# Side steps spaced apart beside a scan, wider rotation over PSUM banks, and delta's ranks computed in four column groups

## The chip, the cores and the metric

The kernel runs on one core of a Trainium2 chip. TensorE (PE) multiplies matrices into PSUM, VectorE (DVE), ScalarE (ACT) and GpSimd (POOL) work on tiles in SBUF (the first two also in PSUM), and SyncE (SP) issues all the DMAs of this kernel on one queue. Each engine runs its instructions in the order in which they stand in its own list and waits, by semaphores, for what other engines make. The metric is the time of one execution on the device in microseconds; lower is better. Runs of the same program are compared by their medians.

## The reference, cut to what matters

Sixteen images of 256 channels and 32 x 32 positions (1024 tokens) pass two layers, each behind a group norm and each with a residual. The first is attention with four heads of 32 and a feed-forward; the second is a gated selective scan with 512 inner channels and 64 states for each.

```python
# layer 0, x += f(gn(x))
tok = gn(x) + pos
q, k, v = split(layernorm(tok) @ w_qkv)
tok = softmax(q k^T * scale) v @ w_out + b_out + tok
tok = gelu(layernorm(tok) @ w_ff1 + b_ff1) @ w_ff2 + b_ff2 + tok
# layer 1, x += f(gn(x)) with pos = rel_h + rel_w added
ctx = sigmoid(conv3(xs) + gate_b)
u, z = split(xs @ in_proj_w.T)
u = silu(causal_depthwise_conv4(u))
dt, Bm, Cm = split(u @ x_proj_w.T, [16, 16 + 64])
delta = softplus(dt @ dt_proj_w.T + dt_proj_b)
h = exp(delta * A) * h + (delta * u) * Bm      # per token, 512 channels x 64 states
y = (h * Cm).sum(states) + u * D
out = (y * silu(z)) @ out_proj_w.T * ctx
```

The recurrence in `h` goes over the 1024 tokens one after another and is the bulk of the arithmetic: 512 x 64 rows of 1024 steps for each image.

## The kernel before, in words

**The scan.** A tile of 128 partitions holds two channels with 64 states each. Tokens are halved into two blocks of 512 (`t`), channels into four groups of 128 (`k`), each into four parts (`q`) of eight units (`i`). So an image has 256 units, and a unit is two scan instructions of 128 x 512 on DVE (`scan`, L893). What a unit needs is made by other engines ahead of it:

- `load` (L842) brings delta times u to all 64 states by DMA, six units ahead, into one of seven buffers `dub`.
- `inputs` (L868) multiplies it by B on POOL (L871), four units ahead.
- `decay` (L873), two units ahead: two PE matmuls (L880) spread three bfloat16 pieces of delta over the states into PSUM tiles `a`, and ACT takes the exponential in place (L883). There are four such tiles, so the matmuls of unit n + 2 write where unit n was read from.
- `outputs` (L917) follows each eight units as a Python generator that is advanced once in every unit: many small PE matmuls (L927) sum h times C over the states into the tile `yb`, ACT copies the half (L935), PE transposes it (L939), ACT copies it again (L947), and four small DMAs (L954) store it in `ys`. The matrix `cd`, made of C, is filled by ACT in `spread_c` (L902).

**The side work.** While image b is scanned, image b + 1 is prepared (`first_norm`, L321; `attention_layer`, L337; `scan_inputs`, L567), and image b - 1 is finished (`gate_and_store`, L773: add u times D, multiply with z, output projection, context gate, residual, store). These are generators too. Each yields a number, its share, after every small step. The main loop (L973) adds a rate to `due` in every unit, and while `due` is positive takes the next step and subtracts its share. The rate is the sum of all shares over the 247 units that may take steps: 247.8 for a preparation, 26.6 more for a gate stage. Whatever is left runs six units before the image ends.

In a unit the loop writes: the load, POOL's product, two scans, the decays of n + 2, side steps, one step of each running `outputs`. At the end of the program (L1022 on) PE, ACT, DVE and POOL are bound to exactly this order by dependencies without semaphores. SP's queue is not bound, and its DMAs stand in the order that the tile framework's scheduler gives them, near this one.

**PSUM.** Eight banks: four for `a` (pool `aps`), one for `yb`, one for the attention's sums `av` (pool `accp`), two for all other products of the side work (pool `mm`). `psum` (L98) hands out the two in turn while a scan runs beside.

**Steps that the change touches.** `group_norm` (L230), `layer_norm` (L271): sums over channels by a matmul with a constant matrix, then Ln and Exp on ACT for the inverse root, then a multiplication on DVE (L267, L306). Scores, softmax and values of attention (L406, L474, L482, L462), projections q and k (L374). z with its tanh (L597 to L617), u with its four taps (L642), the context gate (L651), then dt, B and C (L692 on): for each half of the tokens four accumulating matmuls with 16 columns for dt and four with 128 for B and C. For delta, `begin` multiplies the 16 rows of dt with `w_dt` for each 128 channels (L716), and `begin`, `more` and `rest` make the softplus in small pieces on ACT and DVE (L714 to L765), which ends with three bfloat16 pieces stored to `dps` (L763).

## Time and profile before

| what | us |
|---|---|
| runs shown, median (lowest to highest of 3) | 13563.83 (13536.5 to 13569.5) |
| profiled execution, its own time | 13520.45 |
| its span, first to last instruction | 13518.5 |
| span up to the first scan (image 0 prepared alone) | 376.9 |
| image 0, from its first scan to image 1's | 801.3 |
| image 4, the same | 834.8 |
| from the last image's first scan to its last | 645.4 |
| after the last scan's start | 47.3 |
| busy: DVE, PE, POOL, ACT | 12165.9, 10686.8, 9761.5, 7916.0 |
| scans on DVE (8192 instructions) | 9618.0 |
| mean granted clock of PE, as a share of full | 0.768 |

An engine's busy time is the sum of its instructions; what is left of the span is idle time. In the lists of groups a row has the line, the engine, the operation, the tiles written and read with their sizes, the count, the busy time, the mean of one instruction, and the idle time of the engine just before these instructions with what ended it. In the busy time by windows each row is a stretch of the span, its length, the busy time of PE, PE's weight loads, DVE, ACT and POOL, the granted clock of PE, the share of time in which the DMA engines worked, and GB/s. Matmuls overlap and their ends are modelled, so a PE near its whole window is close to full and no more exact than that.

### The profile page before, as it was taken

How to read it: one execution, taken by the hardware profiler on the slowest of the kernel's cores; microseconds unless marked ns; L12 is line 12 of the kernel's file. 1: busy time of each engine (PE TensorE's matmuls, PEld its weight loads, DVE VectorE, ACT ScalarE, POOL GpSimd, SP SyncE). 2: the span in 40 equal slices, each digit the busy share in tenths (PEclk: the TensorE clock that was granted, in tenths of full speed). 3: DMA queues.
4: the chain of work that ended last, by engine and by line, in shares of the span. 5: the costliest groups of instructions: out<-in, count | busy, mean ns of one | idle time of the engine just before them, and what ended most of it. 6: DMA issues, size and time to landing. Idle time of an engine off the chain costs nothing. (4 is left out here: it accounts for less than half of the span.)

```text
span 13518.5 us, 429250 instructions
## 1 busy us (share of the span) xinstructions
PE 10686.8 (79%) x186800; PEld 5389.6 (40%) x186800; DVE 12165.9 (90%) x11652; ACT 7916.0 (59%) x13941; POOL 9761.5 (72%) x4118
## 2 busy tenths in 40 slices
PE   7787878878787787877878778787787878878767
PEld 3343344433444334443344433434444344433434
DVE  3899999899998999999999898999999999989998
ACT  3666665656655565555656556566465665656654
POOL 0777767777777777767777677776777767777697
PEclk8786877868788686876868778687786877868777
DMA  1566566565665666656666566655666566665666
GB/s 64 202 205 234 197 212 218 203 227 203 208 217 200 228 205 213 212 201 223 208 223 205 198 222 206 235 199 199 220 207 234 193 205 220 206 231 198 209 233 224
DMA packets 1001896, 2820.85 MB, mean 209 GB/s; under 512 B 175810, under 2 KB 319427, under 8 KB 1000004
## 3 DMA queue, kind: packets, MB, share of 16 engines
q1 hardware_dynamic: 1000004, 2793.39, 60.5%
q8 instruction: 1460, 23.92, 0.7%
q14 instruction: 432, 3.54, 0.1%
HBM read 2514.18 MB, written 261.62 MB: 205 GB/s over the span
## 5 line engine op out<-in xcount | busy, mean ns | idle before, releaser
L871 POOL TENSOR_TENSOR dub<-dub,bt 128x1024 f32<-128x1024 f32 x4096 | 9706.4, 2386 | 3702.5 <-DMA dub<-dus 3218.5
L883 ACT ACTIVATE a<-a,acol 128x512 f32<-128x512 f32 x8192 | 5063.6, 659 | 3830.4 <-PE a L880 3800.3
L893 DVE TENSOR_TENSOR_SCAN h<-a,last,dub 128x512 f32<-128x512 f32 x4096 | 4927.0, 1260 | 129.1 <-issue 88.0
L893 DVE TENSOR_TENSOR_SCAN h<-a,dub 128x512 f32<-128x512 f32 x4096 | 4691.0, 1199 | 281.1 <-issue 160.7
L880 PE MATMUL a<-pieces,pick 48*128 48x512 bf16 x8192 | 2983.3, 468 | 2447.9 <-DVE h L893 2371.4
L927 PEld LDWEIGHTS yb<-h,cd 128*32 128x32 f32 x131072 | 2568.5, 136 | 1945.6 <-issue 1700.1
L927 PE MATMUL yb<-h,cd 128*32 128x64 f32 x131072 | 2967.1, 259 | 28.8 <-issue 19.7
L880 PEld LDWEIGHTS <-pick 48*128 48x128 bf16 x8192 | 521.6, 96 | 2607.9 <-issue 2396.6
L406 PE MATMUL s_ps<-k,q 32*64 32x512 f32 x4096 | 890.4, 719 | 59.2 <-DVE mx L387 58.3
L939 PEld LDWEIGHTS yb<-turn,y 128*16 128x16 f32 x32768 | 408.7, 119 | 993.6 <-ACT y L935 493.2
L935 ACT COPY y<-yb 128x256 f32<-128x256 f32 x1024 | 383.3, 374 | 718.3 <-PE yb L927 714.3
L387 DVE TENSOR_REDUCE mx<-s_ps 128x1 f32<-128x512 f32 x1024 | 643.4, 669 | 24.4 <-PE s_ps L406 22.2
L939 PE MATMUL yb<-turn,y 128*16 128x32 f32 x32768 | 538.2, 212 | 103.2 <-ACT y L935 99.4
L474 PE MATMUL st_ps<-sp 33*128 33x512 f32 x2048 | 598.0, 627 | 14.1 <-ACT pt L482 13.9
L462 PE MATMUL av<-pt,vv 128*64 128x512 f32 x2048 | 577.3, 642 | 5.5 <-ACT sums L451 3.3
L482 ACT ACTIVATE pt<-st_ps 128x512 f32<-128x512 f32 x1024 | 556.7, 604 | 40.0 <-PE st_ps L474 38.8
L660 PE MATMUL g_ps<-w,xp 128*128 128x256 f32 x1536 | 447.4, 447 | 0.0
L406 PEld LDWEIGHTS s_ps<-k,q 32*64 32x64 f32 x4096 | 206.8, 148 | 580.1 <-DVE mx L387 540.3
L660 PEld LDWEIGHTS g_ps<-w,xp 128*128 128x128 f32 x1536 | 389.5, 328 | 100.5 <-issue 77.4
L645 DVE SCALAR_TENSOR_TENSOR u<-up,cwh,u 128x1024 f32<-128x1024 f32 x192 | 341.0, 1776 | 32.8 <-ACT u L637 32.5
L819 PE MATMUL m_ps<-w,xs 128*128 128x256 f32 x1024 | 310.4, 451 | 12.3 <-DVE xs L794 12.3
L819 PEld LDWEIGHTS m_ps<-w,xs 128*128 128x128 f32 x1024 | 258.6, 328 | 89.5 <-issue 60.5
(135 smaller groups left out, 7147.0 us busy)
## 6 DMA issues: line engine op xcount, KB each, us to landing
dub<-dus SPq DMA_DIRECT2D x4096, 512.0 KB
dps<-pc SPq DMA_DIRECT2D x384, 128.0 KB
pieces<-dps SPq DMA_DIRECT2D x1024, 48.0 KB
xs<-in_x_dram SPq DMA_DIRECT2D x64, 512.0 KB
xs<-kept SPq DMA_DIRECT2D x64, 512.0 KB
zs<-z SPq DMA_DIRECT2D x64, 512.0 KB
ud<-u SPq DMA_DIRECT2D x64, 512.0 KB
dus<-du SPq DMA_DIRECT2D x64, 512.0 KB
```

Source lines behind the costliest of these rows:

```text
L387: nc.vector.tensor_reduce(mx[:, g, c, hf : hf + 1], s, AX.X, ALU.max)
L406: nc.tensor.matmul(waiting[g][0][ts(e, 64)], q4[r, ts(c, 64)], k4[r, hs(hf)], start=True, stop=True,)
L462: nc.tensor.matmul(av[ts(e, 2 * DH)], vv[j // (NJ // 2)][:, j % (NJ // 2), 2 * pair + e, :], pts[e], start=(j == 0), stop=(j == NJ - 1),)
L474: nc.tensor.matmul(s, ka[r, ts(j, P)], qa[r, hs(hf)], start=True, stop=True)
L660: nc.tensor.matmul(ps[:, ts(q, C)], xp[k][:, ds(first + t, P, 4)], wg_s[:, k, t, :], start=(i == 0), stop=False,)
L819: nc.tensor.matmul(ps[:, ts(q, C)], us[d][:, ds(first, P, 4)], wo_s[:, d, :], start=(d == 0), stop=(d == ND - 1),)
L871: nc.gpsimd.tensor_tensor(v, v, bt.unsqueeze(1).to_broadcast([P, 2, TB]), ALU.mult)
L880: nc.tensor.matmul(a, w, pieces[r], start=True, stop=True)
L883: nc.scalar.activation(a, a, AF.Exp, scale=acol[:, at : at + 1])
L893: nc.vector.tensor_tensor_scan(now["h", q % 2][:, 2 * i + e, :], decays[n][e], loaded[n][:, e, :], first, ALU.mult, ALU.add,)
L927: nc.tensor.matmul(yb[ts(g, 32), ts(s, 64)], cd[:, at // 16, ts(c, 32)], hbuf[:, :, at : at + 4], start=(c == 0), stop=(c == 3),)
L939: nc.tensor.matmul(out4[32 * s : 32 * s + 16, half, e], y2[:, 64 * s + e : 64 * s + 64 : 4], turn[:, e], start=True, stop=True,)
```

## The change

- **Spacing.** The main loop counts `due` down by one in every unit and adds `gap(share, rate)` for each step taken. A share below 1 is a gap in units as it stands; a share of 1 or more becomes the larger of 1 and share/rate, so that no second step falls in its unit. `rate_for` finds the rate by bisection so that all gaps together fill the 247 units; the shares of a preparation are now kept as a list.
- **Other shares.** Nearly all steps have new ones; those of the group norms' multiplications, the additions after them and the fetches and products of `gate_and_store` are 0.4 to 0.6, and the gate stage's shares are the list `GATE`.
- **Distances.** `psum3` takes its tiles in turn from the two banks of `mm` and the one of `accp`; `layer_norm`, z and the output projection use it. In `layer_norm` both means are taken before the first is used. z's product on DVE stands two steps behind its tanh instead of one, and the output projection is finished after the second of its two halves instead of the first.
- **Smaller steps.** A gate step is split by its two blocks of input channels; the product for B and C is split in two; `spread_c` is spread over two units; `outputs` takes one group of matmuls a unit, its transposition follows a unit behind the copy, and its store comes two units later.
- **Ranks.** For dt each of the four blocks of 128 channels gets its own matmul of 32 columns (16 weights and 16 zeros) in its own quarter of the PSUM tile's partitions, without accumulation between them. The sum over the blocks is left to delta's matmul, whose weight `wdt4` repeats `w_dt` in the four quarters, with zeros between, over 128 rows. Both weights are constants loaded once; `w_dt` leaves the per-image weight tile.
- **Constants.** `cd` is allocated and cleared once instead of for every image; `negt` uses a buffer of the `half` pool.

The core of the diff (changes of a share alone, and moved code that the kernel's listing shows, are left out):

```diff
+    three = cycle((mm, mm, accp))
+    def psum3(name):
+        src = next(three) if beside["scan"] else next(alone)
+        return src.tile([P, HL], F32, name=name, tag={mm: "mm", accp: "av"}.get(src, "a"))
...
+    wxd = const.tile([P, ND, 32], F32, name="wxd")
+    nc.gpsimd.memset(wxd, 0.0)
+    wdt4 = const.tile([P, DI], F32, name="wdt4")
+    nc.gpsimd.memset(wdt4, 0.0)
+    for d in range(ND):
+        nc.sync.dma_start(wxd[:, d, :RANK], w_x[ts(d, P), :RANK])
+        nc.sync.dma_start(wdt4[ds(32 * d, RANK)], w_dt)
...
-        m = mean_of([t[:, hs(0)] for t in src], "ln_m")
-        yield 1
-        q0 = centre(0, m)
-        m = mean_of([t[:, hs(1)] for t in src], "ln_m")
-        yield 1.2
-        q1 = centre(1, m)
+        m0 = mean_of([t[:, hs(0)] for t in src], "ln_m")
+        yield 1.3
+        m1 = mean_of([t[:, hs(1)] for t in src], "ln_m")
+        yield 1.3
+        q0 = centre(0, m0)
+        yield 1
         vs = [mean_of(q0, "ln_v")]
+        q1 = centre(1, m1)
         yield 1.2
         vs.append(mean_of(q1, "ln_v"))
-        yield 1
+        yield 1.3
...
-                finish_z()
-                ps = psum("z_ps")
+                finish_z(1)
+                ps = psum3("z_ps")
...
         for hf in range(2):
-            for dst, lo, n in ((dt, 0, RANK), (bc, RANK, 2 * NS)):
-                ps = psum("x_ps", n)
-                for d in range(ND):
-                    nc.tensor.matmul(
-                        ps, wx_s[:, d, lo : lo + n], us[d][:, hs(hf)],
-                        start=(d == 0), stop=(d == ND - 1),
-                    )
-                nc.scalar.copy(dst[:n, hs(hf)], ps)
-                yield 1.6
+            ps = psum("r_ps")
+            for d in range(ND):
+                nc.tensor.matmul(
+                    ps[ts(d, 32)], wxd[:, d], us[d][:, hs(hf)], start=True, stop=True
+                )
+            nc.scalar.copy(dt[:, hs(hf)], ps)
+            yield 1
+            ps = psum("x_ps")
+            for d in range(ND):
+                nc.tensor.matmul(
+                    ps, wx_s[:, d, RANK:], us[d][:, hs(hf)], start=(d == 0), stop=(d == ND - 1)
+                )
+                if d == 1:
+                    yield 1.5
+            nc.scalar.copy(bc[:, hs(hf)], ps)
+            yield 1.5
...
-            nc.tensor.matmul(ps, wdt_s[:, ts(d, P)], dt[:RANK, hs(hf)], start=True, stop=True)
+            nc.tensor.matmul(ps, wdt4[:, ts(d, P)], dt[:, hs(hf)], start=True, stop=True)
...
-    GATE = 26.6
+    GATE = [0.4] * 4 + ([0.6, 0.6, 0.4] * ND)[:-1] + [1.3] * 8 + [1]
...
-                    if q == 0:
+                    if q == 1:
                         finish()
...
+                if s == 3:
+                    y2 = blk.tile([P, 256], F32, name="y2", tag="y2")
+                    nc.scalar.copy(y2, yb[:, :256])
+                if s == 0 and half == 1:
+                    turned(0, y2)
+                if (half, s) != (0, 0):
                     yield
...
+    steps = list(prepare(0))
+    def gap(share, rate):
+        return share if share < 1 else max(1.0, share / rate)
+    def rate_for(shares, room):
+        lo, hi = 0.01, 10.0
+        for _ in range(40):
+            mid = (lo + hi) / 2
+            lo, hi = (mid, hi) if sum(gap(w, mid) for w in shares) > room else (lo, mid)
+        return hi
...
-            due += rate
-            while due > 0.0:
-                due -= next(side, 1e9)
+            due -= 1.0
+            while due <= 0.0:
+                due += gap(next(side, 1e9), rate)
...
-            spread_c(b, t)
+        if (k, q) == (0, 0) and i in (6, 7):
+            spread_c(b, t, ((0, 1), (2, 3))[i - 6])
```

## The prediction

> **What bounds the kernel now.** I read the head of the page first, for the engine whose idle time matters.
>
> ```profile
> PE 10686.8 (79%) x186800; PEld 5389.6 (40%) x186800; DVE 12165.9 (90%) x11652; ACT 7916.0 (59%) x13941; POOL 9761.5 (72%) x4118
> ```
>
> DVE carries two scans per unit and most side work, and the change takes no instruction from it. What can be won is its idle time, the span of 13518.5 less 12165.9: 1352.6 us. The busy time by windows says where that lies. Up to the first scan (376.9 us) DVE works 151.1 us, so 225.8 idle belong to the preparation of image 0. Image 0 takes 801.3 us (57.3 idle), images 1 to 14 about 832 each, the last 645.2 (12.1 idle). One image from the middle, 3674.6 to 4509.4, has 834.8 - 757.5 = 77.3 us idle. I cut it at the borders of its side stages; columns are busy us (and instructions) of each engine, then granted clock, DMA share and GB/s:
>
> ```profile
> 3720.40:3766.00 45.60, 27.44 (x506) 13.78 (x505) 44.49 (x37) 17.70 (x32) 32.36 (x13) 0.52 0.88 313
> 3766.00:3801.50 35.50, 31.59 (x511) 23.89 (x504) 29.79 (x30) 14.13 (x26) 26.62 (x11) 0.88 0.70 251
> ...
> 3953.00:4088.00 135.00, 125.67 (x2471) 60.75 (x2470) 117.41 (x105) 110.38 (x209) 116.58 (x50) 0.93 0.63 218
> ...
> 4222.00:4252.00 30.00, 27.59 (x372) 12.06 (x370) 23.43 (x25) 15.33 (x27) 18.19 (x8) 0.91 0.57 199
> ...
> 4345.00:4374.00 29.00, 25.75 (x442) 12.40 (x434) 22.98 (x22) 20.63 (x36) 18.83 (x8) 0.83 0.56 197
> 4374.00:4486.00 112.00, 78.34 (x1412) 39.48 (x1402) 104.27 (x110) 78.28 (x131) 72.30 (x31) 0.53 0.61 202
> ```
>
> Length minus the third busy figure is DVE's idle time. In the softmax stage (3953 to 4088) PE is busy 125.7 of 135.0 us and DVE 117.4: here PE sets the pace. The same holds for the output projection (from 3766), q and k (3824 to 3841: 15.3 of 17.0), z (4222) and dt/B/C (4345). In delta's stage (4374) no engine is full, so its 7.7 us are waits between engines. The groups of DVE instructions name these (last column: idle just before them, over the whole run):
>
> ```profile
> L729 DVE SCALAR_TENSOR_TENSOR d_ps<-sp_s,d_ps 128x512 f32<-128x512 f32 x128 | 88.4, 691 | 150.3 <-ACT d_ps L725 150.1
> ...
> L306 DVE TENSOR_TENSOR xn<-xn,ln_v 128x512 f32<-128x512 f32 x128 | 81.2, 677 | 105.1 <-ACT ln_v L301 105.1
> ...
> L806 DVE SCALAR_TENSOR_TENSOR m_ps<-xs,m_ps 128x512 f32<-128x512 f32 x64 | 44.5, 695 | 93.7 <-PE m_ps L819 93.7
> ```
>
> Each consumer stands one unit, or none, behind its producer. The timeline shows the other kind of wait, at two projections of q and k in one unit:
>
> ```profile
> 2999.52 5.03 PE L374 MATMUL qk_ps<-xn,w 128*128 128x512 f32 x8
> ...
> 3005.83 1.98 PE L374 MATMUL qk_ps<-xn,w 128*128 128x512 f32 x4
> ...
> 3006.72 2.34 DVE L893 TENSOR_TENSOR_SCAN h<-a,dub 128x512 f32<-128x512 f32 x2 [3.48 <-POOL dub L871]
> ```
>
> Eight matmuls take 5.03 us where a unit of two scans takes 2.34. The decays of the next unit stand behind them in PE's order, and the scan waits 3.48 us. (POOL is named, but the scan's `a` came last: ACT's exponential follows PE's matmul.)
>
> **The change, part by part.** I work in units (two scans, 2.24 to 2.37 us) and put both lists of shares through the loop.
>
> *Spacing.* Before, the rate is 1.11 a unit and two steps of share 1 can fall together. After, such steps stand at least a unit apart; shares over 1.18 are divided by 1.18. Both lists end near unit 245 of 256, so the PE, ACT and DVE totals stay, and the room comes from first_norm and gate_and_store, whose steps are packed.
>
> - q and k: four steps over 5 units instead of 3. PE: 4 x 1.98 + 5 x 1.06 (decays 0.39; outputs (4 x 1.10 + 2 x 0.47)/8 = 0.67) = 13.2 against 11.5 of scans. With the first burst on a slow clock I keep 2.3 of 3.3 us.
> - Softmax and v: about 57 units instead of 51.5. PE: 32 steps x (1.02 + 1.08) + 57 x 1.06 + 3.8 for v = 131.4; DVE 57 x 2.28 = 130. The overhang is 1.4, plus at most the 9.3 that PE did not overlap before: between 1.4 and 10.7 I take 7.5, nearer to the row since steps still come as two in three units. Before: 17.6.
> - Outputs (L927, L939): 1.10 us bursts in four of eight units become 0.55 in six of eight and 1.10 in one, the transposition a unit behind its copy. Same instructions; this is what lets the figure above lie below its upper end. The stores to `ys` go out two units later; an image's last four now stand on SP in unit 10 of the next one, one unit before the first fetch of `ys`, where five lay between.
> - dt/B/C: a full-width group of four costs 1.98, so the eight narrow ones cost 3.96. Four column groups side by side: L927's 64 matmuls of 64 columns took 1.10, 17 ns each against 62 at full width, 3.6 times faster. So 3.96/3.6 = 1.1 and 2 x 2.9 us of PE work go; the rest spreads over 7 units: 2 x 1.1 + 4 x 1.98 + 7 x 1.06 = 17.5 against 16.5 of scans. 6.0 falls to 2.5. Delta's matmul with 128 rows instead of 16 streams the same 512 columns: nothing.
> - z: three banks, a consumer two steps back, 9 units: 8 x 1.98 + 9 x 1.06 = 25.4 against 9 x 2.37 + 8 x 0.68 = 26.8. A slow start remains: 6.6 to 3.0.
> - m_ps: 8 steps over 9 units, finished after the second half. 8 x 2.24 + 9.5 = 27.4 against 26.6, and it begins at the slow clock as now: 5.7 to 4.3.
> - Norms: Ln and Exp stand two units before their consumer. One such pair holds ACT for 5.0 us in layer_norm (two table loads of 1.28, 2 x 0.66, 2 x 0.58); exponentials are due every 2.3, so about 1.5 stays of each 4.0. The two layer norms with neighbours: 5.8 + 4.5 to 2.6 + 2.5; group norms and the feed-forward: 3.8 + 4.9 to 1.8 + 2.0.
> - Delta: `more` and its consumer never share a unit now: the three meetings of 4.0, 1.7 and 1.4 become about 0.9 each. Four blocks of six stores to dps hold SP's order, as before but 7.3 units apart instead of 8.7; dub loads wait behind them and POOL's lead shrinks. I charge 0.7. 7.7 to 4.2.
> - u and gate, the softmax denominators and the scores: 5.8, 3.9 and 0.7 to 2.5, 3.5 and 0.4; the denominators' chain keeps its three units.
>
> *Against it: gate_and_store.* Its first fetch pair stands in units 11 and 12 and the first use of `ud` (L790's operation) in unit 12, where three units lay between. Queued ahead on SP and the DMA are two stores to `kept`, `ys` and two dub loads: 6 x 0.52 MB with its own; at the 384 GB/s of the best ten microseconds here 8.2 us, and DVE arrives 4 us after the first. Behind the waiting instruction stands every later scan. Those last stores to `ys` (1.8 us of SP's time for four in this trace) stand ahead of it too. Bounds 1.1 (as now) and 10; I take 5.0, backlog less arrival and a little for the stores. Later fetches have 8 to 10 us and are covered; w_o leaves this stage because its buffer is free earlier (w_dt is now a constant).
>
> Two rules of the Trainium skill speak against such spacing. L790 costs 2.17 us on average with a minimum of 1.25, and in the last image, where POOL is busy 598 of 645 us, 8.36. "SBUF — State Buffer" (two separate sides) says that VectorE with two SBUF inputs and GpSimd lock a shared port for a whole instruction. By the row of the middle images nothing changes; by the rule each of the 8 packed operations could wait one POOL instruction, 2.39 us more, 19 per image. POOL has gaps there (32.4 of 45.6 us), so I stay with the row. The clock is weighed here:
>
> ```profile
> 3996.18 1.93 PE L927 MATMUL yb<-h,cd 128*32 128x64 f32 x64
> ...
> 4000.65 1.10 PE L927 MATMUL yb<-h,cd 128*32 128x64 f32 x64
> ```
>
> Identical work, granted 0.5 and 1. "TensorE: Matmul & The Clock Gate" (Part 1) says that the clock halves when the engine was not busy lately. By the row each stage keeps its clock; by the rule thinner stages could lose it. Since PE stays above 95% in those computed above, I take the row.
>
> *Small parts.* POOL loses 15 memsets of 3.52 us, hidden by a lead of about 14 us; ACT's eight cd operations (0.40 each) fall in two units, one of them Ln's: within the 1.8. Eight small loads at the start against 5 us of PE work saved in the head: nothing.
>
> **Sum for an image**, before: 3.8 + 1.1 + 5.7 + 5.8 + 3.3 + 0.7 + 17.6 + 3.9 + 4.5 + 4.9 + 6.6 + 5.8 + 6.0 + 7.7 = 77.4. After: 1.8 + 5.0 + 4.3 + 2.6 + 2.3 + 0.4 + 7.5 + 3.5 + 2.5 + 2.0 + 3.0 + 2.5 + 2.5 + 4.2 = 44.1. That is 33.3 saved, 466 over 14 images; image 0 without the gate stage saves half of its 57.3, 29; the last nothing. The profiled execution took 13520.5 us: 13520.5 - 495 = 13025. The median of the runs shown, 13563.8, lies 43 above it: 13070.
>
> **Rivals.**
> - *The waits come back* (0.18). PE's and ACT's lists are as long as before and `a` has only four buffers, so PE can't run ahead; ACT <- PE a 3800 us speaks for it, the certain end of same-unit pairs against it. Saving 10 an image: 13564 - 150 = 13415.
> - *Nearly all goes* (0.10). If only 15 of 77 remain, 62 x 14 + 45 = 913: 12650. The slow-clock starts and the DMA backlog speak against it.
> - *Slower: the clock falls* (0.08). Softmax, z, conv and m_ps hold 265 us of PE work at a mean clock of 0.915. At c it takes 265 x 0.915/c; the gain of 33 is gone at c = 0.81. At 0.75: 58 - 33 = 25 more an image, 13940.
> - *No change* (0.06): the idle time only changes place, 13564.
> - The likeliest, 13070: 0.58.
>
> **Range.** 13500 takes in the second case, 12700 reaches towards the third. No change, slower and most of "nearly all" stay out, some 0.19. A measurement here tells about 0.3% (41 us) from nothing; faster gets 0.58 + 0.18 + 0.10 = 0.86, same 0.06, slower 0.08.
>
> **What would show it.** Right: DVE's busy time unchanged (within 100 us) and its idle time near 860; the idle before L729's, L306's and L806's operations at a third to two thirds; softmax idle of 5 to 10 an image; the idle before L790's operation, 40.0 now, near 95. Wrong: a mean clock well under 0.77, DVE busy time up (the port), or the scans' own wait at 410 as now.

## The result, and the profile after

The kernel after takes 13345.6 us (median of four runs, 13327.3 to 13365.3), the kernel before on the same chip 13562.7: a ratio of 0.984, with a 95% interval of 0.982 to 0.987. It is 217 us faster where 494 were forecast. The range held the time; the sum behind it was wrong by more than half of the gain.

The head of the page after, and the groups of VectorE's instructions (last column: idle time just before them, over the whole run):

```profile
PE 10665.6 (80%) x186800; PEld 5305.6 (40%) x186800; DVE 12217.1 (91%) x11652; ACT 7891.8 (59%) x13941; POOL 9695.2 (73%) x4105
```

```profile
L926 DVE TENSOR_TENSOR_SCAN h<-a,last,dub 128x512 f32<-128x512 f32 x4096 | 4934.2, 1262 | 180.4 <-POOL dub L904 56.0 <-issue 54.8 <-PE yb L967 42.8
L926 DVE TENSOR_TENSOR_SCAN h<-a,dub 128x512 f32<-128x512 f32 x4096 | 4691.0, 1203 | 346.1 <-issue 124.9 <-PE yb L967 105.0 <-POOL dub L904 70.6
...
L666 DVE SCALAR_TENSOR_TENSOR u<-up,cwh,u 128x1024 f32<-128x1024 f32 x192 | 420.6, 2191 | 24.5 <-ACT u L658 24.2
L823 DVE SCALAR_TENSOR_TENSOR xs<-xs,vec 128x1024 f32<-128x1024 f32 x64 | 131.1, 2048 | 133.4 <-DMA xs<-ud 133.4
...
L762 DVE SCALAR_TENSOR_TENSOR d_ps<-sp_s,d_ps 128x512 f32<-128x512 f32 x128 | 88.2, 689 | 54.9 <-ACT d_ps L758 54.9
...
L327 DVE TENSOR_TENSOR xn<-xn,ln_v 128x512 f32<-128x512 f32 x128 | 81.3, 677 | 62.8 <-ACT ln_v L322 62.8
...
L839 DVE SCALAR_TENSOR_TENSOR m_ps<-xs,m_ps 128x512 f32<-128x512 f32 x64 | 43.5, 680 | 14.4 <-PE m_ps L852 14.4
```

Delta's and layer_norm's groups fell within the third to two thirds that was forecast (150.3 to 54.9, 105.1 to 62.8), that of m_ps further (93.7 to 14.4). What came back stands in the other rows. Here are the same scans, tap and gate's product in the profile before, under their old line numbers, and then the denominators' product, before and after:

```profile
L893 DVE TENSOR_TENSOR_SCAN h<-a,last,dub 128x512 f32<-128x512 f32 x4096 | 4927.0, 1260 | 129.1 <-issue 88.0 <-POOL dub L871 38.3
L893 DVE TENSOR_TENSOR_SCAN h<-a,dub 128x512 f32<-128x512 f32 x4096 | 4691.0, 1199 | 281.1 <-issue 160.7 <-POOL dub L871 118.7 <-ACT a L883 0.5
L645 DVE SCALAR_TENSOR_TENSOR u<-up,cwh,u 128x1024 f32<-128x1024 f32 x192 | 341.0, 1776 | 32.8 <-ACT u L637 32.5
L790 DVE SCALAR_TENSOR_TENSOR xs<-xs,vec 128x1024 f32<-128x1024 f32 x64 | 138.6, 2166 | 40.0 <-DMA xs<-ud 40.0
```

```profile
L518 DVE TENSOR_TENSOR ao<-ao,sums 128x512 f32<-128x512 f32 x32 | 39.7, 1242 | 11.3 <-DMA sums<-den 11.2
L539 DVE TENSOR_TENSOR ao<-ao,sums 128x512 f32<-128x512 f32 x32 | 38.7, 1212 | 53.0 <-DMA sums<-den 53.0
```

The scans' own idle time, which the forecast named as the sign of its failure if it stayed at 410.2, rose to 526.5, 147.8 of it behind a name that the rows before don't have: `yb` of `outputs`. The gate's product (L823) waits 133.4 for its transfer, 40.0 before, and the denominators' product 53.0, 11.3 before. And the three products of a tap (L666) last 2191 ns each, 1776 before.

The span went from 13518.5 to 13355.7, by 163: VectorE's idle time fell by 214, and its busy time rose by 51. To see where, I sorted VectorE's idle time of the trace by the unit in which it falls, and took means over the 14 images between the first and the last. In us an image:

| stage (units) | before | after | saved | forecast saving |
|---|---|---|---|---|
| group norm (0-10) | 4.2 | 1.4 | 2.8 | 2.0 |
| gate and store (11-21) | 1.8 | 9.3 | -7.5 | -3.9 |
| m_ps (22-31) | 4.4 | 1.7 | 2.7 | 1.4 |
| layer norm, q and k (32-47) | 10.4 | 5.3 | 5.1 | 4.2 |
| scores (48-79) | 1.3 | 0.2 | 1.1 | 0.3 |
| v and softmax (80-135) | 17.8 | 19.3 | -1.5 | 10.1 |
| denominators (136-146) | 2.0 | 5.8 | -3.8 | 0.4 |
| second norms, feed-forward (147-174) | 9.8 | 5.5 | 4.3 | 4.9 |
| z (175-180) | 5.1 | 0.3 | 4.9 | 3.6 |
| u, dt/B/C, delta (181-255) | 16.7 | 8.1 | 8.5 | 10.3 |
| all | 73.4 | 56.7 | 16.7 | 33.3 |

Three stages miss 19.4 us an image: the softmax 11.6, the denominators 4.2, the gate 3.6. The others together beat the forecast by 2.8. Times 14 that is 232 us too little saved. Image 0 waits 10 us more where 29 less were forecast (39), VectorE works 51 us more, and the head and the last image wait 9 more: 332, which is what the profiled execution lacks of the 495 that were forecast for it.

By windows, stages of the same image of the kernel after, cut at their own borders as the prediction cut those of before (length, then busy us of PE, PEld, DVE, ACT, POOL; granted clock, DMA share, GB/s). The rows are the gate, m_ps, the softmax, z and delta:

```profile
3700.00:3750.21 50.21, 25.20 (x454) 14.85 (x453) 38.27 (x32) 12.90 (x24) 22.14 (x9) 0.56 0.83 292
3750.21:3780.89 30.68, 28.24 (x464) 20.24 (x463) 30.09 (x33) 15.44 (x29) 23.59 (x11) 1.00 0.79 258
3935.16:4082.71 147.55, 135.22 (x2623) 62.49 (x2624) 128.15 (x113) 117.20 (x221) 130.85 (x57) 0.92 0.67 224
4213.41:4234.08 20.67, 20.67 (x362) 9.62 (x361) 20.67 (x23) 14.34 (x26) 13.59 (x7) 1.00 0.73 239
4339.64:4447.63 107.99, 75.35 (x1439) 35.92 (x1442) 103.66 (x110) 85.21 (x142) 76.88 (x33) 0.70 0.68 223
```

In m_ps and z VectorE is now nearly full, and TensorE runs on the full clock. In the gate's stage VectorE stands idle 11.9 of 50.2 us, in the softmax 19.4 of 147.6. The timeline shows one such wait of the softmax, first on VectorE, then what TensorE did meanwhile (start and length in us, engine and line, in brackets the idle time before and what ended it):

```profile
4007.51 6.79 DVE L926 TENSOR_TENSOR_SCAN h<-a,dub 128x512 f32<-128x512 f32 x6 [0.39 <-issue]
4020.49 4.57 DVE L926 TENSOR_TENSOR_SCAN h<-a,dub 128x512 f32<-128x512 f32 x4 [6.19 <-PE yb L967]
```

```profile
4012.11 1.97 PE L483 MATMUL av<-pt,vv 128*64 128x512 f32 x4
4014.02 1.08 PE L967 MATMUL yb<-h,cd 128*32 128x64 f32 x32
4015.03 0.60 PE L913 MATMUL a<-pieces,pick 48*128 48x512 bf16 x2
4015.43 1.91 PE L495 MATMUL st_ps<-sp 33*128 33x512 f32 x4
4017.27 1.97 PE L483 MATMUL av<-pt,vv 128*64 128x512 f32 x4
4019.18 1.08 PE L967 MATMUL yb<-h,cd 128*32 128x64 f32 x32
```

The scans are at the first unit of a block and want to write a state buffer whose last read (L967 at 4019.18) TensorE reaches only at the end of a backlog, all of it on half the clock (av takes 1.97 where it takes 1.08 on the full one). In the order before, the last read stood in step 5 of `outputs`, with three whole units between it and the scans that write the buffer again. In the order after it stands in step 7, with one unit between.

### The profile page after: what moved, and what is told of

It reads as the page before. It is cut to its first block, busy times and chain, and to the rows that moved or that the text cites. A ratio compares the mean times of both kernels' runs of the same rounds, so it can differ in the third digit from the quotient of the medians.

```text
span 13355.7 us, 429794 instructions
## 1 busy us (share of the span) xinstructions
PE 10665.6 (80%) x186800; PEld 5305.6 (40%) x186800; DVE 12217.1 (91%) x11652; ACT 7891.8 (59%) x13941; POOL 9695.2 (73%) x4105
## 5 line engine op out<-in xcount | busy, mean ns | idle before, releaser
L913 PE MATMUL a<-pieces,pick 48*128 48x512 bf16 x8192 | 2941.0, 454 | 2011.5 <-DVE h L926 1929.4
L967 PEld LDWEIGHTS yb<-h,cd 128*32 128x32 f32 x131072 | 2525.7, 131 | 3234.3 <-issue 2194.3
L967 PE MATMUL yb<-h,cd 128*32 128x64 f32 x131072 | 3207.6, 255 | 214.7 <-ACT yo L981 103.1
L427 PE MATMUL s_ps<-k,q 32*64 32x512 f32 x4096 | 830.7, 614 | 97.4 <-DVE mx L408 97.4
L955 PEld LDWEIGHTS yb<-turn,y 128*16 128x16 f32 x32768 | 456.1, 121 | 550.1 <-ACT y L974 305.6
L955 PE MATMUL yb<-turn,y 128*16 128x32 f32 x32768 | 552.1, 215 | 133.7 <-ACT y L974 133.4
L495 PE MATMUL st_ps<-sp 33*128 33x512 f32 x2048 | 625.6, 650 | 0.1
L483 PE MATMUL av<-pt,vv 128*64 128x512 f32 x2048 | 621.9, 688 | 4.6 <-ACT sums L472 3.3
L503 ACT ACTIVATE pt<-st_ps 128x512 f32<-128x512 f32 x1024 | 557.5, 607 | 57.5 <-PE st_ps L495 56.7
L680 PE MATMUL g_ps<-w,xp 128*128 128x256 f32 x1536 | 517.1, 482 | 0.0
L666 DVE SCALAR_TENSOR_TENSOR u<-up,cwh,u 128x1024 f32<-128x1024 f32 x192 | 420.6, 2191 | 24.5 <-ACT u L658 24.2
L852 PE MATMUL m_ps<-w,xs 128*128 128x256 f32 x1024 | 319.0, 461 | 11.9 <-DVE xs L827 11.9
L495 PEld LDWEIGHTS st_ps<-sp 33*128 33x128 f32 x2048 | 222.8, 200 | 195.5 <-issue 109.8
```

Source lines behind the costliest of these rows:

```text
L427: nc.tensor.matmul(waiting[g][0][ts(e, 64)], q4[r, ts(c, 64)], k4[r, hs(hf)], start=True, stop=True,)
L483: nc.tensor.matmul(av[ts(e, 2 * DH)], vv[j // (NJ // 2)][:, j % (NJ // 2), 2 * pair + e, :], pts[e], start=(j == 0), stop=(j == NJ - 1),)
L495: nc.tensor.matmul(s, ka[r, ts(j, P)], qa[r, hs(hf)], start=True, stop=True)
L503: nc.scalar.activation(pt, s, AF.Exp)
L680: nc.tensor.matmul(ps[:, ts(q, C)], xp[k][:, ds(first + t, P, 4)], wg_s[:, k, t, :], start=(k == 0 and t == 0), stop=False,)
L913: nc.tensor.matmul(a, w, pieces[r], start=True, stop=True)
```

## The experiments

Two theories to begin with. Theory 1: the softmax lost its gain to the new order of `outputs`, which lends the state buffers for longer. Theory 2, the rival: TensorE has more work there than the units hold, and which buffer VectorE meets first is of no account.

The runs were taken on several chips, on which the kernel before takes 13525 to 13563 us. Each ratio is to the kernel before on the same chip, with its 95% interval, and small differences between runs are judged by these ratios.

### The order of outputs (e1, e2, e3)

e1 puts the order of before back into the kernel after:

```diff
-                if (half, s) != (0, 0):
-                    yield
-        turned(1, y2)
...
+                if s == 1:
+                    yield
+            y2 = blk.tile([P, 256], F32, name="y2", tag="y2")
+            nc.scalar.copy(y2, yb[:, :256])
+            yield
+            for e in range(4):
+                for s in range(4):
...
+            if half == 0:
+                yield
```

> The kernel after with one part put back: `outputs` computes and turns the y of a block in the order of the kernel before, so the last read of a state buffer stands in step 5 and not in step 7, and VectorE has three units and not one before it writes that buffer again. Theory 1 (the missing gain of the softmax is the new order of `outputs`, which lends the state buffers for two units longer while TensorE lags): the idle time before the scans falls from 526 us to about 400 (390 to 430), what they wait for `yb` from 148 us to under 60, and the time from 13346 to about 13210 us (13170 to 13250). Theory 2 (the softmax waits because TensorE and ScalarE at the granted clock have more work there than its units hold, and which buffer VectorE meets first is of no account): the waits change their names only, to the scores and to the state buffer's first reads, and the time stays within 0.3% of the kernel after.

Measured: 13219.6 us, ratio to before 0.975 (0.973 to 0.976). Its scans:

```profile
L926 DVE TENSOR_TENSOR_SCAN h<-a,last,dub 128x512 f32<-128x512 f32 x4096 | 4930.7, 1263 | 136.6 <-issue 92.9 <-POOL dub L904 40.5
L926 DVE TENSOR_TENSOR_SCAN h<-a,dub 128x512 f32<-128x512 f32 x4096 | 4691.4, 1203 | 295.9 <-issue 164.5 <-POOL dub L904 106.1 <-ACT a L916 20.7
```

`yb` is gone from the releasers and the scans' idle time is 432.5, just above the 390 to 430 that theory 1 gave; the time is the one that it gave. By stage the softmax, where 79.8 of the 147.8 us of waits for `yb` fell, comes down from 19.3 to 14.0, and not to the 7.5 of the forecast. So less than half of its miss goes with this order. The rest of the gain lies in the gate (9.3 to 6.8), in image 0 (68 to 51 us), and in 39 us less busy time.

e2 keeps the new order and reads the buffer one step earlier:

```diff
-                if (half, s) != (0, 0):
+                if (half, s) not in ((0, 0), (0, 2)):
                     yield
...
-        for _ in range(3):
+        for _ in range(2):
+            yield
+        for _ in range(2):
             yield
```

> The kernel after, its new `outputs` with every read of the state buffer one step earlier (the second quarter is computed in the same step as the first): the last read stands in step 6, one unit earlier than in the kernel after and one later than in the kernel before. Theory 1: half to two thirds of what putting back the old order brings, 13260 us (13220 to 13300). Theory 2: within 0.3% of the kernel after.

Measured: 13322.8 us, 0.982 (0.980 to 0.984), within 0.3% of the kernel after, so that the time speaks for theory 2. The stages say something else. The softmax's idle time is 14.0, the same as in e1, and `yb` is no longer among the scans' releasers:

```profile
L926 DVE TENSOR_TENSOR_SCAN h<-a,last,dub 128x512 f32<-128x512 f32 x4096 | 4930.8, 1263 | 135.5 <-issue 96.7 <-POOL dub L904 36.5
L926 DVE TENSOR_TENSOR_SCAN h<-a,dub 128x512 f32<-128x512 f32 x4096 | 4689.7, 1203 | 290.5 <-issue 182.3 <-POOL dub L904 92.1 <-ACT a L916 12.2
```

The gain is spent elsewhere: the gate waits 9.8 and the denominators 6.4 us, and the products of VectorE last longer by 58 us in all than in e1 (one group alone, the addition to `xp`, 82.7 against 51.6 us). One unit less of lending ends the waits for `yb`; that it does not bring the time of e1 was not foreseen by either theory. How much of the new order's cost is the lending itself, and how much the later stores and other meetings of steps, these runs do not separate.

e3 puts the new order alone into the kernel before:

```diff
-                if s == 1:
-                    yield
...
+                if s == 3:
+                    y2 = blk.tile([P, 256], F32, name="y2", tag="y2")
+                    nc.scalar.copy(y2, yb[:, :256])
+                if s == 0 and half == 1:
+                    turned(0, y2)
+                if (half, s) != (0, 0):
+                    yield
+        turned(1, y2)
```

> The kernel before with only the new order of `outputs`. Theory 1: the scans of the softmax meet the state buffer late here too, 5 to 9 us an image: slower, 13640 us (13590 to 13700), idle time before the scans from 410 us to about 490. Theory 2: within 0.3% of the kernel before (13563).

Measured: 13660.0 us, 1.0074 (1.0056 to 1.0092): slower, as theory 1 had it. The scans' idle time is 528.9, above the 490 that it gave:

```profile
L893 DVE TENSOR_TENSOR_SCAN h<-a,last,dub 128x512 f32<-128x512 f32 x4096 | 4926.6, 1262 | 203.9 <-ACT bc L701 76.7 <-issue 59.6 <-PE yb L937 27.5
L893 DVE TENSOR_TENSOR_SCAN h<-a,dub 128x512 f32<-128x512 f32 x4096 | 4693.3, 1203 | 325.0 <-issue 124.6 <-POOL dub L871 101.5 <-PE yb L937 50.9
```

The new order costs 97 us alone, and 126 us beside the rest of the change. Alone it adds 7.5 us of idle time an image, 3.5 in the softmax and 3.3 in the group norm. A part that the forecast counted among the helpers is the largest loss that one edit undoes.

### What the other parts bring alone (e5, e6, e11, e7)

e5 has delta's ranks alone, in the kernel before:

```diff
-            for dst, lo, n in ((dt, 0, RANK), (bc, RANK, 2 * NS)):
+            ps = psum("r_ps")
+            for d in range(ND):
+                nc.tensor.matmul(ps[ts(d, 32)], wxd[:, d], us[d][:, hs(hf)], start=True, stop=True)
+            nc.scalar.copy(dt[:, hs(hf)], ps)
+            yield 1.6
...
-                nc.tensor.matmul(ps, wdt_s[:, ts(d, P)], dt[:RANK, hs(hf)], start=True, stop=True)
+                nc.tensor.matmul(ps, wdt4[:, ts(d, P)], dt[:, hs(hf)], start=True, stop=True)
```

> The kernel before with only delta's ranks side by side in groups of columns (the constants, the smaller buffer of weights and the two kinds of groups in `scan_inputs` go with it); steps and shares stay. Theory 1: TensorE's time in the groups for dt, B and C falls from 233.6 us to about 160, and as it sets the pace in that stage, the stage gives back some 3 us an image: 13515 us (13480 to 13545). Theory 2 (what one stage saves, the next wait takes): within 0.3% of the kernel before.

Measured: 13429.0 us, 0.992 (0.990 to 0.994; the kernel before took 13524.8 on this chip): 96 us, twice what was expected. The groups of TensorE:

```profile
L711 PE MATMUL x_ps<-u,w 128*128 128x512 f32 x256 | 120.1, 612 | 0.0
L704 PE MATMUL r_ps<-u,wxd 128*32 128x512 f32 x256 | 34.1, 605 | 0.0
```

TensorE's time is as expected, 154.2 where it was 233.6. The idle time from unit 181 on falls from 16.7 to 10.4 us an image, 6.3 where 3 were expected: the 79 us less of TensorE's work return at their full size and a little more.

e6 has the new rule alone, that steps of share 1 or more stand a unit apart:

```diff
-            due += rate
-            while due > 0.0:
-                due -= next(side, 1e9)
+            due -= 1.0
+            while due <= 0.0:
+                due += gap(next(side, 1e9), rate)
```

> The kernel before with only the new rule that two steps of share 1 or more stand at least a unit apart; all shares, the order of `outputs`, the banks and the ranks are as before. It takes 0.6 us an image of slack from the other steps (their rate goes from 1.11 to 1.14). Theory 1 (most of the gain is that no two heavy steps share a unit): some half of the 494 us of the forecast, 13330 us (13270 to 13420), with the idle time before the products of delta at under 80 us (150 before). Theory 2 (the longer distances between producers and consumers, which come with new shares, make the gain; the rule alone moves waits): 13520 us (13460 to 13560).

Measured: 13395.0 us, 0.990 (0.988 to 0.992), a gain of 130 us (the kernel before took 13524.8 on this chip too). The time lies in theory 1's range as it stands; but the gain is a quarter of the 494 us and not half, and theory 1's sign, delta's wait under 80 us, failed. z falls from 5.1 to 0.5 us an image and layer norm with q and k from 10.4 to 7.4, but the softmax rises from 17.8 to 19.1, and the product of delta keeps 127.6 us of its 150.3.

e11 is e5 and e6 in one kernel, both diffs above together.

> The kernel before with the rule of the unit between heavy steps and delta's ranks side by side; shares, order of `outputs` and banks as before. Alone they brought 130 and 96 us. Theory 1 (they act in different stages and add up): 13563 - 226 = 13337 us (13295 to 13380), so that the new shares with their longer distances bring the rest, some 120 us, to the 13220 of the kernel after with the old `outputs`. Theory 2 (both take the same waits in the stages of dt, B, C and delta): 13410 us (13385 to 13440), and the new shares bring 190.

Measured: 13367.6 us, 0.986 (0.984 to 0.987): 196 us of the 226 that the two brought alone, in theory 1's range. The step from there to e1 (0.975) is what the new shares, distances and smaller steps bring together: some 1.1%, 150 us.

e7 takes the third bank away from e1:

```diff
-        src = next(three) if beside["scan"] else next(alone)
+        src = mm if beside["scan"] else next(alone)
```

> The kernel after with the old order of `outputs` (measured: 13220 us) and, beside it, layer_norm and z on two banks and not three; shares and distances stay. Theory 1 (the distance of two steps needs the third bank: with two, TensorE's next group waits for VectorE's product of the step before): the idle time before the layer norms' and z's products, 68 + 13 + 10 us there, rises by 40 to 60, and the time to 13275 us (13250 to 13310). Theory 2 (the distances alone do it): within 0.3% of 13220.

Measured: 13206.9 us, 0.976 (0.974 to 0.978; e1: 0.975, 0.973 to 0.976), idle time before the products of z 12.6 us and of the layer norms 68.4 and 12.3, where e1 has 10.2, 67.9 and 13.4. Theory 2: the distances do it, and the third bank brings nothing that can be measured.

### The late transfers (e4, e9, e13)

e4 gives the gate's stage the shares that it had before (the numbers in its `yield` lines, not shown, change in the same way):

```diff
-    GATE = [0.4] * 4 + ([0.6, 0.6, 0.4] * ND)[:-1] + [1.3] * 8 + [1]
+    GATE = [0.7] * 4 + ([1.3, 1.3, 0.7] * ND)[:-1] + [1.3] * 8 + [1]
```

> The kernel after with the shares of the gate and the store at the image's start as they were (0.7 a fetch, 1.3 a product, in place of 0.4 and 0.6), 8 units more for these steps and so 8 fewer for all the others. Theory 1: the wait of the gate's products for their fetches falls from 141 us to about 35, and as the other steps have 8 of 247 units less, 20 to 50 of it come back there: 13275 us (13240 to 13320). Theory 2 (the room is what is short: each unit given here is missed in the softmax): within 0.3% of the kernel after.

Measured: 13429.4 us, 0.990 (0.988 to 0.992), slower than the kernel after by 84 us; neither theory expected that. The gate's idle time falls from 9.3 to 6.0 us an image, all other stages together rise from 47.4 to 55.9. The shares are 7.7 more, but the rate goes from 1.18 to 1.24, so that a share of 1.3 is worth 1.05 units in place of 1.10; the gate's stage gets 5.7 units more and not the 8 of the expectation. Room is the scarce thing: a unit taken from the other steps cost them about 1.5 us an image here. One stage went the other way: the softmax fell from 19.3 to 13.8, with the new order of `outputs` untouched.

So e9, on e1, widens only what stands right ahead of the two waits (the gate's four `yield` lines go from 0.4 to 0.8 with the list):

```diff
-    GATE = [0.4] * 4 + ([0.6, 0.6, 0.4] * ND)[:-1] + [1.3] * 8 + [1]
+    GATE = [0.8] * 4 + ([0.6, 0.6, 0.4] * ND)[:-1] + [1.3] * 8 + [1]
...
             if h % 2 == 1:
-                yield 0.5
-        yield 0.5
+                yield 0.9
+        yield 0.9
+        yield 0.7
         yield 0.5
```

> The kernel after with the old order of `outputs` (13220 us) and 2.6 units more for two chains of transfers, taken from all other steps: the first four fetches of the gate 0.8 of a unit apart in place of 0.4, and 2.5 units in place of 1.5 behind the broadcasts of the denominators. Theory 1 (two late transfers stop VectorE there, 6.8 and 5.0 us an image): 3.3 and 2.5 of these go, and as eight units taken from the other steps cost them some 8.5 us an image in the kernel with the wide gate, 2.6 units cost 2.8: 13220 - 3.0 x 14 = 13180 us (13140 to 13210). Theory 2 (a unit costs elsewhere as much as it saves here): within 0.3% of 13220.

The edit did more than this text says. One `yield 0.5` stayed, so that 3.0 units follow the last broadcasts in place of 1.5, and with the 0.4 between the broadcasts and the 1.6 of the gate the two chains have 3.5 units more, not 2.6.

Measured: 13095.7 us, 0.966 (0.965 to 0.967), the fastest kernel here that leaves nothing out, 250 us ahead of the kernel after. The gain is three times what theory 1 expected (124 us where 40 were): the gate falls from 6.8 to 2.1, the denominators from 5.0 to 0.5, and the give-back of 2.8 did not come (all other stages together: 39.0 before, 36.7 after). Its head, and the two products that waited (for `ud` and for `den`, fetched into `xs` and `sums`):

```profile
PE 10468.1 (80%) x186800; PEld 5277.5 (40%) x186800; DVE 12236.7 (93%) x11652; ACT 7897.1 (60%) x13941; POOL 9720.8 (74%) x4105
...
L824 DVE SCALAR_TENSOR_TENSOR xs<-xs,vec 128x1024 f32<-128x1024 f32 x64 | 127.5, 1992 | 44.1 <-DMA xs<-ud 43.7
...
L540 DVE TENSOR_TENSOR ao<-ao,sums 128x512 f32<-128x512 f32 x32 | 48.2, 1509 | 7.9 <-DMA sums<-den 7.9
```

e13 makes the same edit, 3.5 units here too, in the kernel after with its new order of `outputs`.

> The kernel after (13346 us) with nothing but the wider distances of the two chains of transfers: the gate's first four fetches 0.8 of a unit apart in place of 0.4, and 2.5 units in place of 1.5 behind the broadcasts of the denominators. Beside the old `outputs` that took 124 us. Theory 1 (both transfers are late whatever `outputs` do): the gate's idle time falls from 9.3 to about 4 us an image and that of the denominators from 5.8 to 1: 13346 - 9 x 14 = 13220 us (13180 to 13260). Theory 2 (the four stores of `ys`, which the new order sends two units later, hold these fetches up on SP, so the old order is needed): the gate keeps 7 us and more, 13290 us or more.

Measured: 13227.5 us, 0.977 (0.975 to 0.978): theory 1, at its number. The gate has 4.0 and the denominators 0.9 us an image. The softmax fell too, from 19.3 to 13.6, though nothing was edited there, as in e4. A likely reason, not tested, is that its steps now meet the blocks of eight units at other places. The waits for `yb` stay, at 91.6 of 147.8 us (us in total, times, longest):

```profile
DVE h L927 <- PE yb L968: 91.6, 79, 2.9
```

So what the late last read costs the softmax is not fixed. The loss by the new order as a whole hardly changes: between e13 and e9 it is 1.1% of the time before, between the kernel after and e1 1.0%. Between e13 and e9 it is spread: 3.4 us an image in the stages from u to delta, 1.8 in the gate, 1.1 in z, 0.9 in the softmax, and 12 us once in the head.

### What is left of the softmax's wait (e8, e12, e14, e15)

e8, on e1, gives the softmax 6.4 units more, which it takes from the steps of the scores:

```diff
                     to_space.pop(0)()
-                yield 1
+                yield 0.8
...
-                    yield 1.75
+                    yield 1.98
```

> The kernel after with the old order of `outputs` (measured: 13220 us) and 6.4 units more for the softmax: the steps of the scores, where VectorE waits for nothing (0.3 us an image), stand 0.8 of a unit apart in place of 1, and the softmax's 1.98 / 1.18 = 1.68 units in place of 1.48. In the kernel with the old order the 48 units of the softmax hold 114 us of TensorE against 109 of VectorE; with 54.4 units it is 121 against 124. Theory 1 (TensorE's work per unit is what the softmax waits for): its idle time falls from 14.0 us an image to about 7, and the time to 13120 us (13080 to 13170). Theory 2 (the waits there are stretches on half the clock, which come whenever TensorE has gaps, so more room brings more of them): 13 to 16 us of idle time stay, 13220 us within 0.3%.

Measured: 13254.3 us, 0.979 (0.977 to 0.981), a little slower than e1. The softmax does fall, from 14.0 to 9.8 us. But the scores, which waited for nothing, now wait 7.0: two of their steps can share a unit, and then the maxima stand right behind their matmuls (us in total, times, longest):

```profile
DVE mx L408 <- PE s_ps L427: 117.6, 117, 9.0
```

The room was not free, and the gain was spent where it was taken. Theory 1 is right on the softmax and wrong on the sum.

e12, on e1, leaves out every second product with the values:

```diff
                 def values(j):
+                    if j % 2:
+                        pts.clear()
+                        return
...
-                            start=(j == 0), stop=(j == NJ - 1),
+                            start=(j == 0), stop=(j == NJ - 2),
```

> The kernel after with the old order of `outputs` (13220 us) where every second block of keys is left out of the products with the values (part of the attention is not computed): TensorE has 16 x 1.05 = 17 us an image less in the softmax, ScalarE and VectorE the same. Theory 1 (TensorE's work per unit, 114 us in 48 units against VectorE's 109, makes the softmax's waits): 97 against 109, idle time there from 14.0 us an image to 4 to 7, time 13110 us (13070 to 13150). Theory 2 (half-clock stretches behind TensorE's gaps make them, and more gaps bring more such stretches): 11 us and more stay, 13180 us or more.

Measured: 13223.2 us, 0.975 (0.973 to 0.976), the time of e1. Seventeen microseconds of TensorE's work an image are gone from its busiest stage, and nothing is gained: the softmax waits 15.8 us where it waited 14.0. The same 48 units of one image by windows, e1 first:

```profile
3911.34:4034.20 122.86, 113.89 (x2256) 51.61 (x2254) 109.32 (x98) 100.53 (x192) 110.83 (x49) 0.93 0.71 234
```

```profile
3912.59:4038.87 126.28, 111.29 (x2200) 54.61 (x2196) 109.61 (x96) 101.21 (x193) 112.26 (x49) 0.84 0.66 226
```

TensorE is busy 111.3 us with less to do where it was busy 113.9, and the granted clock is 0.84 where it was 0.93. By the clock's records in the trace, the softmax (units 84 to 135, mean of the 14 images) spends 35.9 us on the half clock, in 6.6 stretches, where e1 spends 15.8 us in 3.3. That is what the second theory says: work that is taken away leaves gaps, and gaps take the clock.

If that were all, added work would do no harm. e14 and e15 add some, on e9:

```diff
+            for _ in range(2 if 80 <= n % UNITS < 136 and i < 2 else 1):
                 nc.tensor.matmul(a, w, pieces[r], start=True, stop=True)
```

> The kernel with the old `outputs` and the wider fetches (13096 us) with added work: in 14 of the 56 units of the softmax, where TensorE waits for VectorE most (the first two units of each block), it computes the decays of a unit twice, 0.39 us each time, 5.5 us an image. Theory 1 (gaps bring the half clock, and the half clock brings the waits): fewer such stretches than the 2.3 an image now, and the time falls to 13060 us (13030 to 13085) though the work grows. Theory 2 (TensorE's work is what waits): 2 to 5 us an image more, 13130 us (13110 to 13170).

Measured: 13116.8 us, 0.968 (0.967 to 0.970; e9: 0.966, 0.965 to 0.967), not to be told from e9. The number lies in theory 2's range, but the softmax moved as theory 1 says, a little: it waits 11.6 us where it waited 12.7, with 2.0 half-clock stretches where there were 2.4. 5.5 us of work an image in TensorE's gaps cost the softmax nothing, and win nothing that can be measured.

e15 adds work elsewhere:

```diff
+                        for _ in range(2 if e == 1 and j % 2 else 1):
                             nc.tensor.matmul(s, ka[r, ts(j, P)], qa[r, hs(hf)], start=True, stop=True)
```

> The kernel with the old `outputs` and the wider fetches (13096 us) with added work: in every second step of the softmax TensorE computes the scores of one of the two heads twice, 16 x 0.51 = 8.2 us an image. Theory 1: the work fills gaps and so keeps the clock; half-clock stretches fall below 2.3 an image and the time stays within 0.3% of 13096. Theory 2: the softmax gets longer by what is added, 13096 + 8.2 x 14 = 13210 us (13170 to 13250).

Measured: 13337.5 us, 0.984 (0.982 to 0.986). 49 us of the 242 more lie ahead of the first scan, where image 0 does the same work with nothing beside it; the softmax's idle time rises from 12.7 to 27.5 us an image. Beside the softmax's own steps, 8.2 us of work cost 14.8: theory 2, and more than it said. The half clock did not become rarer, as theory 1 has it: it takes 20.6 us of the same units, 11.2 in e9.

Taken together: the stage has about as much work for TensorE as for VectorE. Less work cost clock (e12), more work in the heavy steps cost waits and clock (e15), more work in the gaps cost nothing (e14). I take it that a wait in one unit isn't made good in the next because the decays run only two units ahead; no run had more buffers for them, so this is not shown. How the 12 to 14 us that are left divide between half-clock stretches and pairs of heavy steps is not settled by these runs.

### The longer products (e10)

e10 takes POOL's products out of the kernel after:

```diff
-        nc.gpsimd.tensor_tensor(v, v, bt.unsqueeze(1).to_broadcast([P, 2, TB]), ALU.mult)
+        del v, bt
```

> The kernel after without POOL's 4096 products of `dub` and B, so that the scans read the transferred tile (this part of the computation is left out) and POOL does next to nothing. Theory 1 (VectorE's operations with two operands in SBUF last longer than their shortest because POOL runs beside them): the three products of a tap (mean 2191 ns, shortest 1250) and the gate's (2048 and 1816) come down to about 1250 each, VectorE's busy time falls from 12217 by some 340 to about 11880 us (11840 to 11960), and with POOL's own 127 us of waits the time to about 12880 us (12780 to 13000). Theory 2 (they are slowed by the transfers that write SBUF meanwhile, or by nothing that POOL does): busy time over 12150 us, time over 13150.

Measured once: 13007.3 us. Its head and two of the groups:

```profile
PE 10595.5 (81%) x186800; PEld 5283.6 (41%) x186800; DVE 11880.6 (91%) x11652; ACT 7885.4 (61%) x13941; POOL 4.8 (0%) x9
...
L666 DVE SCALAR_TENSOR_TENSOR u<-up,cwh,u 128x1024 f32<-128x1024 f32 x192 | 243.5, 1268 | 23.5 <-ACT u L658 23.3
...
L823 DVE SCALAR_TENSOR_TENSOR xs<-xs,vec 128x1024 f32<-128x1024 f32 x64 | 81.9, 1279 | 146.8 <-DMA xs<-ud 146.5
```

VectorE's busy time falls by 336.5 us to the number that theory 1 gave (11880), the tap's product from 2191 to 1268 ns and the gate's from 2048 to 1279. The transfers are still there, so they are not the cause. The time falls by 338 and not by 470, to just outside theory 1's range. VectorE's idle time stays (1138.6 us after, 1124.9 here): the waits that had the names of POOL and `yb` stand behind ScalarE's operations, 295.0 us behind its decays alone.

## Why the prediction was wrong

The direction and most stages were right. The size failed: three terms were mis-sized (outputs and softmax together, the gate, image 0), and two were put at next to nothing (the denominators and the longer products, below as the port).

*Outputs.* The step said "Same instructions; this is what lets the figure above lie below its upper end". It counted the length of a burst and not how long the state buffer stays lent. The last read moved two steps later, and in the timeline above TensorE runs about a unit late. The new order as a whole cost 1.0 to 1.1% of the time, some 130 us beside the other parts (e1, e9 against e13), and 97 alone (e3). The lending shows in it by name: the scans' waits for `yb` are 147.8 us in the kernel after, 91.6 in e13, 78.4 in e3, none in e1 and e9. That it is the whole of the loss is not shown, as e2 ends these waits and gains only some 23 us. The kernel before could have told: with two buffers, the distance from the last read to the next write is the slack of everything that TensorE does in between.

*Softmax.* "Between 1.4 and 10.7 I take 7.5" came out as 19.3, 162 us of the miss. Putting the old order back takes 5.3 of the 11.8 away (e1), and so do shifts of the steps with the new order in place (e4, e13). The step that failed for the other 6.5 is the sum itself: it set all of TensorE's work in the stage (131.4) against all of VectorE's (130) and took the difference. e12 takes 17 us of that work away and wins nothing, e15 adds 8.2 and loses 14.8. Waits like the one in the timeline are made within two or three units, and means over 50 do not see them. What exactly makes the rest is open.

*Gate.* 5.0 us was forecast, with 10 as the upper bound; it measured 9.3. The mechanism was right, a fetch too close to its use: 1.6 units more ahead of the product take most of the wait away (e9, e13). The stores ahead of it on SP can be no more than a part: with the old order, which sends those to `ys` earlier, the gate still waits 6.8 (e1). The term was mis-sized. I had taken VectorE's arrival, 4 us, off a backlog of 8.2; a likely reason, not tested, is that the stage ahead of it lost 2.8 us of waits, so that VectorE comes sooner.

*Denominators.* "The denominators' chain keeps its three units" failed in its last link. From the reciprocal to the product it keeps its length (four units in both traces, in the image that the prediction cut), but from the last broadcasts to the product the lists leave 2.4/1.11 = 2.2 units before and 1.5 after. VectorE's wait for the broadcasts went from 11.3 to 53.0 us, and with 3.0 units it is 7.9 (e9).

*Image 0.* The 29 us to be saved there were half of its idle time, with no working behind them. It waits 10 us more; with the old order of `outputs` it waits 17 less than that (e1).

*The port.* I took the row of the gate's product (2.17 us, to stay) over the rule of the Trainium skill, "SBUF — State Buffer" (two separate sides), that VectorE with two SBUF inputs and GpSimd lock a port for a whole instruction. For that row the forecast held, 2166 to 2048 ns. But the taps, of the same kind, went from 1776 to 2191 ns, 80 us in all, and after what other groups gave back VectorE's busy time rose by 51. The trace agrees with the rule. Of the 192 products of a tap, 125 begin while POOL works, and 124 of these end 1.09 us on average behind POOL's instruction, whatever was left of it: they last 2.69 us on average, the free ones 1.26. Before, 124 began so and lasted 2.04. There are no more meetings, only longer ones. e10, a single run, puts the whole price at 336 us, more than the change brought.

*The clock.* Taking the row over the rule was right for the mean: 0.768 before, 0.790 after; m_ps went from 0.88 to 1.00, z from 0.91 to 1.00. In the softmax it stayed where it was (0.93 and 0.92), and e12 shows it falling there when TensorE has less to do.

*What was right, or better than forecast.* Spacing ended the pairs in one unit: m_ps, z, layer norms, q and k saved 12.7 us an image where 9.2 were forecast; e6 shows 130 us from the rule alone. The ranks were taken at 3.5 us an image and measured 6.3 alone (e5). z got its distance, but not from the third bank (e7). Delta and u were taken 1.8 us too well.

*The rivals.* The time lies 69 us below "the waits come back" (13415) and 276 above the likeliest. That rival's reason, that TensorE cannot run ahead with four buffers of decays, fits the softmax, but no run tested it; in seven of the ten stages the waits did not come back. The 33.3 us an image that were to be saved were 16.7.

## What to carry to other kernels

When an edit moves the last read of a buffer, count the distance to the next write, not only the work that moves: here a new order with the last read two steps later, on two buffers, cost 1% of the time. When steps are spread over a fixed number of slots, a slot can have a price elsewhere (e4, e8), so widen only what stands right ahead of a wait: 3.5 units in the right two places gave 0.8 and 0.9% (e13, e9), 5.7 over one whole stage cost 0.6% (e4). In a stage where two engines are equally full, the difference of their sums forecast little here; look at two or three neighbouring units.

## What was not expected of the hardware

Less work on TensorE left the time as it was (e12), and more of that work ran on half the clock. In the trace after, the granted clock is full or half, in stretches that are multiples of 3.41 us. Its slices of 3.41 us, sorted by how busy TensorE was in the 3.41 us ahead of each: below 65%, 912 of 967 slices are on the half clock; from 65 to 95%, 591 of 1475; above, 140 of 1456. So with some 1.2 us of gaps or more in 3.41, the half clock followed in 94 of 100 slices.

An engine that is off the critical path set the length of another's instructions: POOL cost VectorE 336 us of busy time (e10), nearly all of it in products with two operands in SBUF, and it stands in the profile as longer instructions, not as a wait.
